# Four convolution layers on 16 images: how the last stage recomputes and loads what it needs

## The chip, the core and the metric

The kernel runs on one core of one Trainium2 chip. Its engines are TensorE (PE, matrix products, with a separate row PEld for its weight loads), VectorE (DVE), ScalarE (ACT), GpSimd (POOL) and SyncE (SP); here POOL and SP mainly issue transfers. The metric is the device time of one execution in microseconds (us). A profile is taken of one execution: its span runs from the first to the last instruction, and the execution's own time is a little longer than its span.

## The reference

The input x has 16 images of 64 channels and 128x128 points, in float32. Four layers follow, each a residual on a group-normalised input:

```python
x = x + L0(gn(x))   # gram matrix of the channels, applied to the image, then a 64x64 mix
x = x + L1(gn(x))   # |Scharr x| + |Scharr y|, per channel
x = x + L2(gn(x))   # temporal shift, 3x3 convolution 64 -> 64, bias
x = x + L3(gn(x))   # 3x3 convolution, 1x1 convolution + b, batch norm, leaky ReLU, clip
```

with, in the last one (called x3 below is its input, y its convolution's output):

```python
y = conv(conv(gn(x3), w_bin), w1x1) + b1x1
mean, var = mean(y, axis=(0, 2, 3)), var(y, axis=(0, 2, 3))     # over all 16 images
y = (y - mean) * rsqrt(var + 1e-5) * gamma + beta
out = x3 + clip(where(y >= 0, y, 0.1 * y), 0, 255)
```

The clip at 0 makes the leaky part a plain ReLU. The mean and the variance need y of every image before the first output can be written; so the kernel has a last stage.

## The kernel before

**The main loop.** Images go through the layers as a pipeline, in chunks of R = 8 rows per half image (a half image has 64 rows; channels of the upper half sit on 64 partitions, of the lower half on the other 64). A step of the loop (`for step in range(FIRST - 2, steps)`) handles a pair of chunks of layer 2 or layer 3 of some image, beside the front layers of a later one. Within a step, `ORDER` is a list, written out by hand, of named pieces of work, and each engine gets its instructions in that order; the wrapper `InOrder` keeps the order of the program (all instructions carry its line, L134, in the profile, so rows are told apart by tile names). `planned` says which step is which; `last_one` is the last step with layer 3 in it.

**What layer 3 leaves behind.** `Layer3.combine` sums y into `bn_sum`, and `Layer3.square` its squares into `bn_sq`. For most images `Layer3.store` writes y to memory (`y_d`), 32 transfers per image from SP. For the images in `AGAIN` y is not stored: the last stage convolves x3 again. x3 is stored for all images (`x3_d`), for those in `AGAIN` as two halves, and their normalising coefficients are kept in `kept`.

**The last stage.** `todo` is a list of 128 pieces. A *loaded* piece is an eighth of an image, whole: y and x3 are read (two transfers of 512 KB), y is scaled, shifted and passed through a ReLU on ScalarE, `min(., 255) + x3` is done on VectorE, and the result is written by POOL. A chunk *again* is one chunk of an image in `AGAIN`: only x3 is read (512 KB), normalised on ScalarE (`again_in`, with the border row above; `again_close`, with the border row below, which comes from the next chunk's x3 or from `xe`, a few rows read ahead), convolved on TensorE (`again_products`), and finished by `again_out`.

`again_products` uses weights that already hold the 1x1 convolution (`w3`, from which `rows_of[ky, h]` are views). The array is used as four quadrants of 64x64: two row halves h times two groups g of four output rows. Nine taps (ky, kx) times four quadrants give 36 products of 4 rows, 512 columns (508 for the outer kx), into the PSUM tile `two_again` (two banks, two buffers). In the profile each product has two records and each record its own weight load. `again_out` then reads the sums on ScalarE (ReLU with scale and shift into z, in three pieces, since the second group's halves lie crossed), adds on VectorE and sends two transfers of 256 KB from POOL.

**Landing places.** Buffers that the main loop no longer needs are collected in `room` (37 places of 512 KB over the run). `fetch` takes the next piece of `todo`, one place or two, and issues its loads from SP. It is called from the last steps of the main loop on, and in the last stage while more than 8 places are free. A load into a place waits for the write out of it.

**Order around the change.** When the main loop is done, `mv`, two small products into `bank` and a chain of small VectorE instructions make the scale `sc` and the shifts `sh` and `shb`. In between stands the first `again_in`. Then the loop over `todo` begins: two chunks with eight loaded pieces, then chunks and loaded pieces mixed, and the last six pieces loaded ones.

Of the kernel before, what the change touches and what calls it, by code (L numbers as in the profile page):

```python
# [80 lines left out]
    ],  # L81
}
FIRST, LAG = 15, 10
AGAIN = (3, 4, 5, 6, 7, 8)
CP = 4
GN_EPS = 1e-5
BN_EPS = 1e-5
# [83 lines left out]
def tile_kernel(ctx: ExitStack, tc: tile.TileContext, x, cw_h, w2_t, b2, wbin_t, w1_t, b1, gamma, beta, consts, out):  # L171
# [58 lines left out]
    def cols(o):  # L230
        return slice(o * C, (o + 1) * C)
# [27 lines left out]
    def chunk_tile(name):  # L259
        return ring.tile([P, (R + 2) * W], F32, tag="v", name=name, bufs=4)  # L260
# [879 lines left out]
    def start_of(b):  # L1140
        return FIRST + LAG + NS * b
# [32 lines left out]
    N = R * W  # L1174
    parts = deque((b, q) for b in range(B) if b not in AGAIN for q in range(C * HW // P // N))
    again = deque((b, i) for b in AGAIN for i in range(NS))
    todo, ahead, behind = [], 8, 6
    share = len(parts) - ahead - behind
    for n in range(NS * len(AGAIN)):
        todo.append(("again",) + again.popleft())  # L1180
        while n > 0 and len(todo) - n - 1 < ahead + (n - 1) * share // (NS * len(AGAIN) - 2):
            todo.append(("loaded",) + parts.popleft())
    todo += [("loaded",) + part for part in parts]
    room, loaded, at_hand = deque(), deque(), deque(maxlen=2)

# [39 lines left out]
    def again_in(b, i, t):  # L1225

        n = AGAIN.index(b)
        v = v_again[0].rearrange("p (j w) -> p j w", w=W)
        v_again.rotate(1)
        r = t.rearrange("p (j w) -> p j w", w=W)  # L1230
        if i == 0:
            act.copy(v[lo, 0, :], w0[lo])
            again_norm(n, v[hi, 0, :], xe[hi, n], hi)
        else:
            again_norm(n, v[:, 0, :], at_hand[-1][1][:, R - 1, :])
        again_norm(n, v[:, 1:R + 1, :], r)
        at_hand.append((v, r, b, i))

    v_again = deque()

    for step in range(FIRST - 2, steps):
        now[0] = step
# [39 lines left out]
        for name in ORDER[kind_of(step)]:  # L1282
            if name in acts:
                if acts[name]:
                    acts[name]()
                continue
            if name == "section":
                if stage:
                    section_of_pair()
                section()  # L1290
                continue
            if name in PARTS:
                for b in fronts:
                    run(Front, b, step - FIRST - NS * b, name)
                continue
            phase[0] = q = int(name)
            for b in range(1, B):
                at, n = pace[b]
                if n == 1:
                    run(Gram, b, step - at, q)  # L1300
                elif 0 <= step - at <= 5:
                    live.setdefault((Gram, b), Gram(b)).half(4 * (step - at) + q)

            first = FIRST
            if step == first and q < 3:
                rows_to_columns(1, NS - 3 + q, rows[NS - 3 + q])
            if q == 1 and first + 2 <= step < first + 5:
                weights_of_layer_3(step - first - 2)
            if q == 1 and step == first + 5:
                other_weights()  # L1310
            tick()

            if step == start_of(B - 1) and q == 0:
                slices(xw.rearrange("p w c t -> p (w c t)"), 8)
                slices(xh.rearrange("p a j w -> p (a j w)"), 3)
                rest(xin, "x", [R, W], 2)
                rest(xin, "xr", [C // 8, W], 3)
# [22 lines left out]
    v_again.extend(chunk_tile(f"v_again_{n}") for n in range(2))  # L1340
    rest(ring, "y", [2, CP, W], 2)
    for t in (dA, dB[0], dB[1]):
        slices(t.rearrange("p n j w -> p (n j w)"), 1)
    rest(ring, "v", [(R + 2) * W], 4, 2)
    while len(room) > 1 and fetched[0] < len(todo):
        fetch()

    mv = cpool.tile([P, 2], F32, name="mv")
    dve.tensor_reduce(mv[:, 0:1], bn_sum, axis=AX.X, op=ALU.add)
# [34 lines left out]

    rows_of = {(kk, i): w3[cols(i), slot, :, cols(o)] for slot, i, o, kk in TO_PAIRS}
    def again_close(r_next):

        v, _, b, i = at_hand[-1]  # L1390
        n = AGAIN.index(b)
        if i + 1 == NS:
            act.copy(v[hi, R + 1, :], w0[hi])
            again_norm(n, v[lo, R + 1, :], xe[lo, n], lo)
        else:
            again_norm(n, v[:, R + 1, :], r_next[:, 0:W])

    def again_products():

        v, r, b, i = at_hand[-1]  # L1400
        two = ps_two.tile([P, 2, CP, W], F32, tag="two", name=f"two_again_{b}_{i}")
        order = [(ky, kx) for kx in (1, 0, 2) for ky in range(3)]
        for n, (ky, kx) in enumerate(order):
            o0, o1 = (0, W) if kx == 1 else (1, W) if kx == 0 else (0, W - 1)
            for g in range(2):
                for h in range(2):
                    j = g * CP + ky
                    pe.matmul(
                        two[cols(h if g == 0 else 1 - h), g, :, o0:o1], rows_of[ky, h][:, kx],
                        v[cols(h), j:j + CP, o0 + kx - 1:o1 + kx - 1], start=n == 0, stop=n + 1 == len(order),  # L1410
                    )
        summed.append((two, r, b, i))

    def again_out():

        two, r, b, i = summed.popleft()
        to = out[b].rearrange("c h w -> (c h w)")
        for g in range(2):
            z = ring.tile([P, CP * W], F32, tag="c", name=f"z_{b}_{i}_{g}", bufs=2)
            for o, at in ((slice(0, P), slice(0, P)),) if g == 0 else ((lo, hi), (hi, lo)):  # L1420
                act.activation(z[o], flat(two[at, g]), AF.Relu, bias=shb[at], scale=sc[at, 1:2])
            to_rows = flat(r[:, g * CP:(g + 1) * CP, :])
            dve.scalar_tensor_tensor(to_rows, z, 255.0, to_rows, op0=ALU.min, op1=ALU.add)
        for h in range(2):
            pool.dma_start(halves(to, h, i * R, R), flat(r)[cols(h)])
        room.append(flat(r))

    rows_of = {(kk, i): w3[cols(i), slot, :, cols(o)] for slot, i, o, kk in TO_PAIRS}
    summed, coming = deque(), deque()
# [23 lines left out]
    while summed:  # L1453
        again_out()


# [36 lines left out]
```

## Time and profile before

| | us |
|---|---|
| median of 3 runs (2513.69 to 2517.16) | 2515.8 |
| the profiled execution's own time | 2513.39 |
| its span | 2511.6 |
| PE busy in the span | 2409.6 (96%) |
| DVE busy | 2078.0 (83%) |
| ACT busy | 2083.6 (83%) |
| POOL busy | 699.5 (28%) |
| last instruction of the main loop's products begins | 2103.6 |
| first product of the last stage begins | 2111.3 |
| end of the span | 2511.6 |

The last stage is thus some 400 of 2511.6 us. Its times below are counted from the span's start. In rows of groups, "x3456 | 375.5, 593" means 3456 instructions, in all 375.5 us during which at least one ran, 593 ns each; what follows is the time that the engine stood idle before them, and who ended that. Matmuls run several at once, so their durations do not add up to time. In rows of a stretch, "20.00 (x108)" is an engine's busy time and count there. "PEclk" or the granted clock is the share of its full clock that TensorE had. A DMA row gives the issuing queue and the time from issue to landing.

### The profile page before, as it was taken

The numbers are of one execution on the slowest core, as the hardware profiler recorded it, in microseconds if no ns is written. First come the engines' busy times: TensorE is split into PE (matmuls) and PEld (weight loads), VectorE is DVE, ScalarE is ACT, GpSimd is POOL, SyncE is SP. The second block draws the span as 40 slices with busy tenths as digits, with TensorE's granted clock in tenths as the row PEclk, the third lists the DMA queues.
The fourth block names the chain that finished last, engine by engine and source line by source line (L and its number), as shares of the span: only waits on it lengthen the run. The fifth ranks groups of instructions, "written<-read, shape, count | busy, mean of one in ns | idle before, by whom it ended". The sixth has DMA issues, their size and how long they took to land.

```text
span 2511.6 us, 52876 instructions
## 1 busy us (share of the span) xinstructions
PE 2409.6 (96%) x19286; PEld 936.2 (37%) x19286; DVE 2078.0 (83%) x2811; ACT 2083.6 (83%) x3509; POOL 699.5 (28%) x1254
## 2 busy tenths in 40 slices
PE   7588999999999999999999999999999999999996
PEld 5333343334334343434343434343333332333332
DVE  4998999999999999999999999999999534444333
ACT  4777999999898898898989899988898656778775
POOL 3251313131423232323323232323232201222222
PEclk8688999999999999999999999999999999999998
DMA  8777888887868686858686978786877798999998
GB/s 229 196 191 205 217 221 224 220 221 197 189 178 199 166 210 163 210 160 207 165 212 183 240 202 233 203 214 160 212 188 174 181 257 277 418 417 418 417 410 338
DMA packets 610579, 585.35 MB, mean 233 GB/s; under 512 B 48480, under 2 KB 521984, under 8 KB 610320
## 3 DMA queue, kind: packets, MB, share of 16 engines
q1 hardware_dynamic: 556752, 425.34, 60.6%
q0 software_dynamic: 53568, 156.63, 20.6%
q8 instruction: 153, 2.51, 0.4%
q14 instruction: 106, 0.87, 0.1%
HBM read 321.46 MB, written 243.28 MB: 225 GB/s over the span
## 4 chain that ended last, share of the span: by engine, by line
PE 77%; DMA 9%; DVE 8%; ACT 2%; issue 2%; POOL 1%; SPq 1%; DVEq 0%; ACTq 0%; POOLq 0%
PE two L134 35%; PE one L134 23%; PE two_again L134 9%; PE bank L134 5%; PE po L134 4%; DVE u L134 3%; DMA end_x<-x_d 3%; DVE e L134 2%; DMA xw<-x_d 1%; DMA v<-x_d 1%; PE pg L134 1%; DMA end_e<-x_d 1%; DMA dA<-x_d 1%; DMA xw<-y_d 1%; DMA xh<-x_d 1%
## 5 line engine op out<-in xcount | busy, mean ns | idle before, releaser
L134 PE MATMUL two<-dA,w 64*64 64x512 f32 (+2 forms) x2304 | 532.8, 595 | 0.0
L134 PE MATMUL two_again<-v_again,w 64*64 64x508 f32 (+1 forms) x3456 | 375.5, 593 | 10.3 <-ACT v_again L134 10.3
L134 PE MATMUL one<-v,w 128*64 128x508 f32 (+2 forms) x1600 | 360.4, 583 | 0.3 <-ACT c L134 0.3
L134 PE MATMUL two<-dB,w 64*64 64x512 f32 (+2 forms) x1536 | 354.6, 594 | 0.0
L134 POOL DMA_DIRECT2D v<-x_d x480 | 238.2, 502 | 399.2 <-PE bank L134 143.7
L134 PE MATMUL one<-v,wi 128*64 128x508 f32 (+3 forms) x1536 | 344.1, 581 | 0.7 <-ACT c L134 0.6
L134 DVE SCALAR_TENSOR_TENSOR e<-e 128x1032 f32<-128x1032 f32 (+1 forms) x256 | 312.8, 1222 | 0.0
L134 ACT ACTIVATE xh<-po,co 128x128 f32<-128x128 f32 (+1 forms) x480 | 274.9, 623 | 25.1 <-PE po L134 24.9
L134 PEld LDWEIGHTS two<-dA,w 64*64 64x64 f32 (+1 forms) x2304 | 150.3, 133 | 287.9 <-issue 283.8
L134 PEld LDWEIGHTS two_again<-v_again,w 64*64 64x64 f32 x3456 | 127.3, 134 | 257.8 <-issue 239.0
L134 ACT ACTIVATE v<-x,co 128x1024 f32<-128x1024 f32 (+3 forms) x256 | 205.3, 847 | 4.0 <-POOL co L134 4.0
L134 PE MATMUL po<-x,abd 64*64 64x512 f32 (+1 forms) x1024 | 179.4, 621 | 21.1 <-ACT xh L134 19.0
L134 PEld LDWEIGHTS one<-v,w 128*64 128x64 f32 x1600 | 109.7, 137 | 211.5 <-issue 187.3
L134 POOL DMA_DIRECT2D q<-dB x128 | 66.6, 522 | 425.4 <-PE one L134 110.9
L134 PEld LDWEIGHTS one<-v,wi 128*64 128x64 f32 x1536 | 103.9, 135 | 215.5 <-issue 171.3
L134 DVE SCALAR_TENSOR_TENSOR y<-two,c 128x1024 f32<-128x1024 f32 x128 | 155.9, 1218 | 32.8 <-PE two L134 23.1
L134 ACT ACTIVATE v<-v,co 128x1154 f32<-128x1154 f32 x128 | 172.0, 1344 | 13.3 <-DMA v<-x_d 11.0
L134 DVE TENSOR_TENSOR dB<-v 128x1024 f32<-128x1024 f32 (+1 forms) x128 | 151.9, 1187 | 36.5 <-ACT v L134 30.9
L134 PE MATMUL two<-q,cross 64*64 64x512 f32 (+1 forms) x768 | 177.2, 570 | 2.2 <-DMA q<-dB 1.5
L134 PE MATMUL two<-dA,wi 128*64 128x508 f32 (+1 forms) x768 | 174.9, 589 | 0.0
L134 DVE TENSOR_TENSOR dA<-v 128x1024 f32<-128x1024 f32 x128 | 156.1, 1219 | 19.3 <-ACT v L134 18.0
L134 DVE SCALAR_TENSOR_TENSOR u<-e,co,u 128x1024 f32<-128x1024 f32 x128 | 164.1, 1282 | 5.3 <-DVE u L134 0.5
(228 smaller groups left out, 4331.4 us busy)
## 6 DMA issues: line engine op xcount, KB each, us to landing
x_d<-u SPq DMA_DIRECT2D x256, 256.0 KB, 3.1
x_d<-x SPq DMA_DIRECT2D x490, 128.0 KB, 4.1
xr<-in_x SPq DMA_DIRECT2D x120, 512.0 KB, 5.8
y_d<-y SPq DMA_DIRECT2D x320, 128.0 KB, 3.9
x<-in_x SPq DMA_DIRECT2D x128, 256.0 KB, 4.9
x<-in_x POOLq DMA_DIRECT2D x128, 256.0 KB, 4.8
end_x<-x_d SPq DMA_DIRECT2D x36, 512.0 KB, 18.1
xw<-x_d SPq DMA_DIRECT2D x33, 512.0 KB, 13.5
```

The source lines that it names most:

```text
L134: return self.tc.keep_in_program_order(call(*args, **kwargs))
```

## The change

Seven images are in `AGAIN` instead of six, so the last stage has 56 chunks and 72 loaded pieces (before 48 and 80), and image 9's y is neither stored nor read.

`again_products` makes two output rows of five products instead of six: with weights w0, w1, w2 of the three rows of taps and input rows v0 to v3, w1(v1 + v2) serves both rows; row 0 adds w0 v0 + (w2 - w1) v2, row 1 adds (w0 - w1) v1 + w2 v3. The row sums v1 + v2 (`s_again`) are made by VectorE in `again_in`, the weight differences (`apart_again`, in `wm`) once by POOL. Each product has 2 rows, 256 columns (254). The shared product goes to banks of its own (`ones`, one in `ps_one`, one in `ps_po`). `again_evict` copies it to SBUF on ScalarE (`c_again`, one buffer in the space of `dA`); `again_sum` adds it on VectorE to the other sums, into z; `again_out` makes the ReLU from z in place.

The order is changed too. The first chunk's `again_in` stands in the step after `last_one`, its products directly behind the two small products of the statistics. `todo` begins with two chunks, then mixes 60 loaded pieces evenly with the chunks, and ends with twelve loaded pieces. At a chunk k the loop does: close and products of k-1, sums of k-2, input of k, copies of k-1, output of k-2; at a loaded piece only that piece's work, except at the end. `dA` is no longer a landing place.

```diff
-AGAIN = (3, 4, 5, 6, 7, 8)
+AGAIN = (3, 4, 5, 6, 7, 8, 9)
...
-    todo, ahead, behind = [], 8, 6
-    share = len(parts) - ahead - behind
+    todo, behind = [], 12
+    share = len(parts) - behind
     for n in range(NS * len(AGAIN)):
+        while len(todo) - n < (n - 1) * share // (NS * len(AGAIN) - 2):
+            todo.append(("loaded",) + parts.popleft())
         todo.append(("again",) + again.popleft())
-        while n > 0 and len(todo) - n - 1 < ahead + (n - 1) * share // (NS * len(AGAIN) - 2):
-            todo.append(("loaded",) + parts.popleft())
...
         again_norm(n, v[:, 1:R + 1, :], r)
         at_hand.append((v, r, b, i))
+        dve.tensor_add(s_again[0], v[:, 1:R + 1:2, :], v[:, 2:R + 2:2, :])
...
             if step == last_one - 3 and q == 0:
+                apart_again = wm.rearrange("p k (n c) -> p n k c", n=2)
+                for h in range(2):
+                    for n, ky in enumerate((2, 0)):
+                        pool.tensor_sub(apart_again[cols(h), n], rows_of[ky, h], rows_of[1, h])
...
+            if step == last_one + 1 and q == 0:
+                v_again.extend(chunk_tile(f"v_again_{n}") for n in range(2))
+                aside = dA.rearrange("p n j w -> p (n j w)")
+                s_again.append(aside[:, 0:CP * W].rearrange("p (j w) -> p j w", w=W))
+                c_again.append(aside[:, CP * W:2 * CP * W])
+                again_in(*todo[0][1:], loaded[0][0])
...
-    for t in (dA, dB[0], dB[1]):
+    for t in dB:
...
     pe.matmul(pm[:, 2:4], k("same"), mv, start=True, stop=True)
+    again_close(loaded[1][0])
+    again_products()
...
-    again_in(*todo[0][1:], loaded[0][0])
...
     def again_products():
...
-        order = [(ky, kx) for kx in (1, 0, 2) for ky in range(3)]
-        for n, (ky, kx) in enumerate(order):
+        s = s_again[0]
+        for part in range(5):
+            for kx in (1, 0, 2):
...
+                        if part == 0:
+                            dst, wt, of = ones[g][to, 0:2], rows_of[1, h], s[cols(h), 2 * g:2 * g + 2, at]
+                        else:
+                            n, far = divmod(part - 1, 2)
+                            dst = two[to, g, n:n + 3:2]
+                            wt = rows_of[2 * n, h] if far else apart_again[cols(h), n]
+                            j += ((2, 0), (1, 3))[n][far]
+                            of = v[cols(h), j:j + 3:2, at]
...
+    def again_evict():
+        while evicted:
+            filled.append(c_again[0])
+            for g, one in enumerate(evicted.popleft()):
+                act.copy(c_again[0][:, 2 * g * W:2 * (g + 1) * W], flat(one[:, 0:2]))
+
+    def again_sum():
+        two, r, b, i = summed.popleft()
+        c = filled.popleft()
...
+                dve.tensor_add(
+                    z[o].rearrange("p (j t w) -> p j t w", t=2, w=W),
+                    two[at, g].rearrange("p (j t) w -> p j t w", t=2),
+                    c[at, 2 * g * W:2 * (g + 1) * W].rearrange("p (j w) -> p j w", w=W).unsqueeze(2)
+                    .to_broadcast([P if g == 0 else C, 2, 2, W]),
+                )
...
     def again_out():
...
-                act.activation(z[o], flat(two[at, g]), AF.Relu, bias=shb[at], scale=sc[at, 1:2])
+            act.activation(z, z, AF.Relu, bias=shb, scale=sc[:, 1:2])
...
         if way == "again":
             (t,) = loaded.popleft()
-            if n > 0:
+            if n > 1:
                 again_close(t)
                 again_products()
-                coming.append((b, q, t))
+            if len(summed) > 1:
+                again_sum()
+            if n > 0:
+                again_in(b, q, t)
+            again_evict()
+            if summed_up:
+                again_out()
         else:
...
-            if len(summed) > 1 or summed and n > len(todo) - behind + 1:
+            if n > last_again and n != last_again + 2 and summed:
+                again_sum()
+            again_evict()
+            if summed_up:
                 again_out()
-            if coming:
-                again_in(*coming.popleft())
-            elif n == len(todo) - behind + 1:
+            if n == last_again + 1:
                 again_close(None)
                 again_products()
```

More of the change, by code (lines that the diff above doesn't have):

```diff
@@ L1237, in again_in @@
         at_hand.append((v, r, b, i))
-    v_again = deque()
+        dve.tensor_add(s_again[0], v[:, 1:R + 1:2, :], v[:, 2:R + 2:2, :])
+    v_again, s_again, c_again = deque(), deque(), deque()
+    rows_of = {(kk, i): w3[cols(i), slot, :, cols(o)] for slot, i, o, kk in TO_PAIRS}
     for step in range(FIRST - 2, steps):
@@ L1339, in tile_kernel @@
         tick()
-    v_again.extend(chunk_tile(f"v_again_{n}") for n in range(2))
     rest(ring, "y", [2, CP, W], 2)
-    for t in (dA, dB[0], dB[1]):
+    for t in dB:
         slices(t.rearrange("p n j w -> p (n j w)"), 1)
@@ L1346, in tile_kernel, with again_close, again_products @@
         fetch()
+    def again_close(r_next):
+        v, _, b, i = at_hand[-1]
+        n = AGAIN.index(b)
+        if i + 1 == NS:
+            act.copy(v[hi, R + 1, :], w0[hi])
+            again_norm(n, v[lo, R + 1, :], xe[lo, n], lo)
+        else:
+            again_norm(n, v[:, R + 1, :], r_next[:, 0:W])
+    def again_products():
+        v, r, b, i = at_hand[-1]
+        two = ps_two.tile([P, 2, CP, W], F32, tag="two", name=f"two_again_{b}_{i}")
+        ones = [
+            pool_of.tile([P, CP, W], F32, tag=tag, name=f"one_again_{b}_{i}_{tag}")
+            for pool_of, tag in ((ps_one, "one"), (ps_po, "po"))
+        ]
+        s = s_again[0]
+        for part in range(5):
+            for kx in (1, 0, 2):
+                o0, o1 = (0, W) if kx == 1 else (1, W) if kx == 0 else (0, W - 1)
+                at = slice(o0 + kx - 1, o1 + kx - 1)
+                for g in range(2):
+                    for h in range(2):
+                        to, j = cols(h if g == 0 else 1 - h), g * CP
+                        if part == 0:
+                            dst, wt, of = ones[g][to, 0:2], rows_of[1, h], s[cols(h), 2 * g:2 * g + 2, at]
+                        else:
+                            n, far = divmod(part - 1, 2)
[3 more added lines that the diff above has]
+                            of = v[cols(h), j:j + 3:2, at]
+                        pe.matmul(
+                            dst[:, :, o0:o1], wt[:, kx], of,
+                            start=part < 2 and kx == 1, stop=part in (0, 4) and kx == 2,
+                        )
+        evicted.append(ones)
+        summed.append((two, r, b, i))
@@ new lines, in again_evict @@
+    def again_evict():
[6 more added lines that the diff above has]
+        c = filled.popleft()
+        zs = []
+        for g in range(2):
+            z = ring.tile([P, CP * W], F32, tag="c", name=f"z_{b}_{i}_{g}", bufs=2)
+            for o, at in ((slice(0, P), slice(0, P)),) if g == 0 else ((lo, hi), (hi, lo)):
+                dve.tensor_add(
[3 more added lines that the diff above has]
+                    .to_broadcast([P if g == 0 else C, 2, 2, W]),
+                )
+            zs.append(z)
+        summed_up.append((zs, r, b, i))
@@ new lines, in again_out @@
+    def again_out():
+        zs, r, b, i = summed_up.popleft()
+        to = out[b].rearrange("c h w -> (c h w)")
+        for g in range(2):
+            z = zs[g]
+            act.activation(z, z, AF.Relu, bias=shb, scale=sc[:, 1:2])
+            to_rows = flat(r[:, g * CP:(g + 1) * CP, :])
+            dve.scalar_tensor_tensor(to_rows, z, 255.0, to_rows, op0=ALU.min, op1=ALU.add)
+        for h in range(2):
+            pool.dma_start(halves(to, h, i * R, R), flat(r)[cols(h)])
+        room.append(flat(r))
@@ L1348, in tile_kernel @@
+    summed, summed_up, evicted, filled = (deque() for _ in range(4))
     mv = cpool.tile([P, 2], F32, name="mv")
@@ L1383, in tile_kernel @@
     dve.scalar_tensor_tensor(shb, sc[:, 1:2], b1_sb, sh[:, 1:2], op0=ALU.mult, op1=ALU.add)
[L1387 to L1401, printed above, removed]
-        order = [(ky, kx) for kx in (1, 0, 2) for ky in range(3)]
-        for n, (ky, kx) in enumerate(order):
[L1404 to L1420, printed above, removed]
-                act.activation(z[o], flat(two[at, g]), AF.Relu, bias=shb[at], scale=sc[at, 1:2])
[L1422 to L1429, printed above, removed]
+    last_again = max(n for n, (way, _, _) in enumerate(todo) if way == "again")
     for n, (way, b, q) in enumerate(todo):
@@ L1452, in tile_kernel @@
             fetch()
-    while summed:
-        again_out()
 def kernel(x, L0_conv_conv_w, L2_conv_W, L2_conv_b, L3_conv_w_bin, L3_conv_w1x1, L3_conv_b1x1, L3_conv_gamma,
```

## The prediction

> **What bounds the kernel now.** I read the page's line of granted clock first, then the end of the run in stretches, then the chain of work that ended last, then single rows for prices.
>
> The stretches (columns: span, length, busy time of each engine with its count, granted clock, DMA share, GB/s):
>
> ```profile
> 2060.00:2080.00 20.00, 20.00 (x108) 6.47 (x106) 9.14 (x12) 8.20 (x13) 0.00 (x0) 1.00 0.88 222
> ...
> 2100.00:2120.00 20.00, 13.94 (x80) 4.87 (x80) 10.09 (x26) 13.79 (x19) 2.23 (x4) 0.74 0.91 283
> ```
> ```profile
> 2120.00:2400.00 280.00, 280.00 (x2628) 94.34 (x2624) 116.51 (x129) 222.08 (x281) 68.78 (x127) 1.00 1.03 417
> 2400.00:2480.00 80.00, 78.30 (x730) 27.87 (x723) 29.77 (x35) 59.80 (x75) 18.99 (x35) 1.00 1.02 409
> 2480.00:2500.00 20.00, 8.48 (x60) 2.28 (x54) 8.71 (x9) 10.82 (x14) 4.85 (x9) 0.82 0.94 359
> ```
>
> From 2112 on, TensorE and the DMA engines are both full: 280.00 of 280 us, and 417 GB/s, which no stretch exceeds. VectorE is 42% busy there, ScalarE 79%. The chain says which of the two full resources ends last (start, length, what):
>
> ```profile
> 2111.26 218.38 PE two_again L134 x2016
> ...
> 2330.87 16.38 DMA end_x<-x_d
> 2347.29 0.03 issue
> 2347.32 18.08 DMA end_x<-x_d
> ...
> 2467.65 16.56 DMA xw<-y_d
> ```
>
> TensorE leads until 2330; afterwards it is a row of loads, up to a loaded piece that arrives at 2484 and lets the last products start. The last combine on VectorE (a loaded piece's) ends at 2503.47, and 8.1 us later the span is over. So before ends by DMA, with TensorE some 10 to 15 us behind it. Before the stage, TensorE is full (20.00 of 20), which hides what the change does there.
>
> **1. Products.** Removed: per chunk 36 products of 512 (508) columns, recorded twice, 72 instructions in 18 rounds of four quadrants. Added: 60 products of 256 (254) columns, 30 rounds. A round now takes 0.427 us (bursts of four weight loads start at 2489.57, 2490.00, 2490.43), a chunk 18 x 0.427 = 7.68. For narrow products the near row is the closing of layer 2, products of 127 and 128 columns, each with its own weight load, two quadrants at a time:
>
> ```profile
> 1927.58 0.82 PE L134 MATMUL two<-v,wi 128*64 128x128 f32 x12
> ...
> 1929.54 2.73 PE L134 MATMUL one<-v,w 128*64 128x512 f32 x12
> ```
>
> 36 of them lie between these starts: 1.96 us, 18 pairs of 0.109. That is 0.85 ns a column against 0.83 in the wide rounds, so 256 columns take about 0.215 and a chunk 30 x 0.215 = 6.45. Sum: 56 x 6.45 = 361.2 against 48 x 7.68 = 368.6.
>
> A rule speaks against this. The Trainium skill, "TensorE: Matmul & The Clock Gate", section on packing small matmuls, says that a weight load overlaps running matmuls only where the row group differs. All four quadrants are streaming when the next four loads run (133 ns each), so by the rule a round would cost its stream plus 0.133: today's chunk 18 x 0.560 = 10.1, the new one 30 x 0.348 = 10.4. The trace has 7.68, so here the loads are covered; I take 6.45. The same page's section on the back-to-back gap gives 81 ns a product at 128 columns in a stream with loads, where the isolated gap would be 56. The closing row has no such surcharge, but it has two loads in flight, not four: upper end 0.25 a round, 7.5 a chunk.
>
> **2. Start.** The first chunk's norms and its row sum move one step ahead of the statistics, ScalarE and VectorE being idle there (6.79 us before the last evictions), and its products follow the two statistics products. These end at 2108.15; the first product starts there rather than at 2111.26. The statistics chain keeps its order. TensorE still idles from 2104.2 to 2107.1, so the halved clock remains (0.74 in the stretch above). In before it cost 218.38 - 28 x 7.68 = 3.3 us; I take 3.0, between 2.8 and 4.5. Last product: 2108.15 + 3.0 + 361.2 = 2472.4, where before had 2494.
>
> **3. ScalarE and VectorE.** Removed per chunk: three ScalarE reads of the product banks (0.79 apart: 2.37 for three). Added: two ScalarE copies 128x256, two Relu 128x512 in place, three VectorE sums (one 128x512, two 64x512 that cross the halves) and one row sum. Prices:
>
> ```profile
> L134 ACT COPY xw<-turned 128x512 f32<-128x512 f32 x8 | 4.7, 588 | 20.0 <-DVE xw L134 20.0
> L134 ACT COPY w<-bank 64x192 f32<-64x192 f32 x6 | 1.9, 316 | 2.6 <-PE bank L134 2.5
> L134 ACT ACTIVATE v<-x,co 128x512 f32<-128x512 f32 x16 | 12.8, 802 | 0.0
> L134 ACT ACTIVATE z<-two_again,shb,sc 64x512 f32<-64x512 f32 x96 | 74.3, 774 | 1.9
> ```
> ```profile
> L134 DVE SCALAR_TENSOR_TENSOR xw<-z,xw 128x512 f32<-128x512 f32 x24 | 16.4, 690 | 14.7 <-ACT z L134 14.6
> L134 DVE TENSOR_TENSOR dB<-v 128x768 f32<-128x768 f32 x16 | 15.3, 956 | 2.6 <-ACT v L134 2.6
> ```
>
> A copy of 256 lies between 316 and 588: 0.37. Successive ScalarE starts are 0.10 closer than a duration (2142.59, 2142.98 for a 0.48), VectorE's 0.08 to 0.09. Where the partition half changes there is no such overlap (the z rows). So: copy 0.27 to the next start, Relu 0.71, a loaded Relu 1.13, norms 0.39 + 1.13 + 0.39; sums 0.70 each, row sum 0.61, combines 0.61 and 1.14. With 60/56 loaded pieces per chunk ScalarE needs 5.1 of 6.45 and VectorE 5.2. By count neither is the bound.
>
> By waits they come close. The copies are queued on ScalarE in front of the Relus and the loaded piece's Relu, and they wait for a buffer that exists once: the second copy of chunk k-1 for the sums of k-2, which stand on VectorE behind the last loaded combine, which waits for the loaded Relu, which stands behind the copies. One turn of this loop: 0.04 + 0.27 + 2 x 0.71 + 1.23 + 0.03 + 1.14 + 2.10 = 6.23. Where two loaded pieces follow each other (6 times in 54) it is 1.14 more, mean 6.36. TensorE wants the copies only some 3.6 us later than they come, so a single long turn is absorbed. TensorE sets the pace, by 0.1.
>
> A chunk's next border row is needed only by the last fifth of its products. At the end the last chunk's border stands behind the Relus of the chunk before, 3.9 us after that one's products, in time for the last fifth at 5.2.
>
> **4. DMA.** Image 9 is no longer read from the stored convolution: 8 pieces of 0.524 MB, at 417 GB/s 10.1 us. One buffer (dA) is no longer a landing place: one piece less in advance, 1.3 us back. Net 8.8. In the main loop 32 stores and their SP issues go, under a full TensorE. Two border loads more on SP (12 took 7.5 us, so 1.3) lie there too, as do four subtractions on POOL: its 64x192 copies took 1235 ns, so 5 to 10 us, while POOL has no instruction in 2060 to 2080. If that cover failed it would cost those few us. The order that spreads loaded pieces evenly fills the eight-place reserve more slowly; during that DMA is not full, but before had the like at its end, so I put the net at nothing (-3 to +4).
>
> **5. Tail.** After the last product: sums to 2.35, the Relu to 3.2, the first of nine loaded Relus to 4.3, then nine combines of 1.14: 14.7, to 2487.1, and 8.1 to the end: 2495. By DMA: 2511.6 - 8.8 = 2502.8. DMA is later and decides. The profiled execution itself took 2513.39 and the median of the runs is 2515.8; so the forecast is 2515.8 - 8.8 = 2507.0.
>
> **The rivals.**
> *ScalarE and VectorE set the pace (slower).* The loop over the one copy buffer. For it: the margin is 0.1 us, and no row shows a copy of 256 or a crossing sum. With copies at 0.41, Relus and sums at 0.79: 0.04 + 0.41 + 1.58 + 1.26 + 0.06 + 1.14 + 2.37 = 6.86, mean 7.0, 56 x 0.54 = 30 us behind TensorE's own time: 2525, median 2529. It decides once the mean turn passes 6.45 + (2511.6 - 2495)/56 = 6.74. Against: each row lies near the lower values.
> *Weight loads show (slower).* At 0.25 a round 56 x 7.5 = 420: 2554, median 2558. It eats the gain from 0.225 a round on. Against: the closing row.
> *Cancelling.* A mean turn of 6.65 to 6.8, or a DMA start that is slower by 5 us or more: 2511 to 2521.
> *TensorE's path alone decides (faster still).* The loads run ahead: 2495, median 2499. Against: 417 GB/s is already full.
>
> **How the numbers follow.** Forecast 0.48, TensorE's path 0.06, cancelling 0.18, the loop 0.20, weight loads 0.08. About 0.2% (5 us) is what a measurement of this kernel tells from no change. Faster 0.54, same 0.18, slower 0.28. The likeliest case alone spans 2502 to 2511 (DMA start, clock). The range gives up most of the loop's upper end and the weight loads: 2500 to 2530.
>
> **What would show it.** Rounds of 0.215 and a chunk pitch of 6.45 with TensorE full; a pitch of 6.7 or more with TensorE waiting for the copy or the row sum means the loop; longer rounds at full clock mean the weights. First product near 2108. DMA near 417 GB/s from about 2140 on. The last combine a loaded piece's, near 2490 to 2495. The prediction is wrong if a copy, Relu or sum costs a tenth more than its row, since 56 turns multiply it.

## The result, and the profile after

| | before | after |
|---|---|---|
| median of 18 runs each, us | 2513.59 (2510.55 to 2519.43) | 2520.23 (2516.33 to 2524.51) |
| ratio after / before, 95% interval | | 1.0025 (1.0018 to 1.0033) |
| the profiled execution's own time, its span | 2513.39, 2511.6 | 2520.33, 2518.5 |
| the two statistics products begin | 2107.1 | 2111.1 |
| from there to the end of the span | 404.5 | 407.4 |
| bytes moved in that time (from the trace) | 162.2 MB | 158.0 MB |

The changed kernel is 6.6 us slower; the forecast was 8.8 us faster. It moves 4.2 MB less in its last stage and still needs 2.9 us more for it.

The page of the changed kernel, head and busy times: TensorE has less to do than before (2409.6 us), VectorE 154 us more, ScalarE 13 us more.

```profile
span 2518.5 us, 59953 instructions
...
PE 2396.1 (95%) x22550; PEld 1066.5 (42%) x22550; DVE 2231.9 (89%) x3043; ACT 2096.2 (83%) x3607; POOL 709.3 (28%) x1267
```

The last stage in stretches (span, length, busy time and count of PE, PEld, DVE, ACT, POOL, then granted clock, DMA share, GB/s):

```profile
2100.00:2120.00 20.00, 17.05 (x178) 8.66 (x180) 7.70 (x23) 9.44 (x17) 0.64 (x1) 0.91 0.97 297
2120.00:2140.00 20.00, 20.00 (x379) 14.23 (x372) 16.70 (x22) 16.50 (x25) 4.70 (x9) 1.00 0.96 319
2140.00:2160.00 20.00, 20.00 (x378) 14.24 (x374) 16.75 (x23) 17.02 (x27) 5.17 (x10) 1.00 1.00 368
2160.00:2180.00 20.00, 20.00 (x380) 14.26 (x376) 16.86 (x23) 17.23 (x27) 5.47 (x10) 1.00 1.03 415
2180.00:2200.00 20.00, 20.00 (x380) 14.26 (x376) 16.86 (x23) 15.72 (x25) 4.93 (x9) 1.00 1.03 415
2200.00:2400.00 200.00, 200.00 (x3732) 142.53 (x3728) 167.95 (x221) 169.51 (x261) 52.54 (x96) 1.00 1.03 411
2400.00:2480.00 80.00, 74.31 (x1387) 52.69 (x1376) 66.51 (x87) 64.79 (x98) 21.35 (x39) 0.98 1.02 408
2480.00:2500.00 20.00, 0.00 (x0) 0.00 (x0) 7.54 (x7) 7.91 (x7) 4.31 (x8) 0.50 0.99 405
```

TensorE is full until 2474, and in the last 44 us it has nothing to do, while the transfers go on at 405 GB/s. So transfers decide the end, as forecast (experiment 4 bears it out). But three things in the last column differ from before, where the stretches from 2120 to 2400 had 417, 417, 417, 418, 417: a slow start (319 and 368), then 411 where 417 stood, and the drain is longer.

The end, on VectorE: each of the last combines (start, length, what; in brackets the idle time before and who ended it) waits for its load.

```profile
2501.71 1.23 DVE L134 SCALAR_TENSOR_TENSOR end_xr<-end_e,end_xr 128x1024 f32<-128x1024 f32 x1 [4.08 <-DMA end_xr<-x_d]
2505.45 1.22 DVE L134 SCALAR_TENSOR_TENSOR end_x<-end_xr,end_x 128x1024 f32<-128x1024 f32 x1 [2.52 <-DMA end_x<-x_d]
2508.46 1.23 DVE L134 SCALAR_TENSOR_TENSOR q<-end_u,q 128x1024 f32<-128x1024 f32 x1 [1.79 <-DMA q<-x_d]
```

### The profile page after: what moved, and what is told of

Its sections match the earlier page's. It is cut to its first block, busy times and chain, and to the rows that moved or that the text cites. A ratio compares the mean times of both kernels' runs of the same rounds, so it can differ in the third digit from the quotient of the medians.

```text
span 2518.5 us, 59953 instructions
## 1 busy us (share of the span) xinstructions
PE 2396.1 (95%) x22550; PEld 1066.5 (42%) x22550; DVE 2231.9 (89%) x3043; ACT 2096.2 (83%) x3607; POOL 709.3 (28%) x1267
## 4 chain that ended last, share of the span: by engine, by line
PE 82%; DVE 8%; DMA 4%; issue 2%; ACT 2%; POOL 1%; SPq 1%; DVEq 0%; POOLq 0%; ACTq 0%
PE two L134 36%; PE one L134 23%; PE two_again L134 11%; PE bank L134 4%; PE po L134 4%; DVE u L134 3%; PE one_again_one L134 3%; DVE e L134 2%; DMA v<-x_d 1%; DMA q<-dB 1%; PE pg L134 1%; DMA y_d<-y 1%; SPq L134 1%; DVE dB L134 1%; DVE dA L134 1%
## 5 line engine op out<-in xcount | busy, mean ns | idle before, releaser
L134 DVE SCALAR_TENSOR_TENSOR u<-xh,co,u 128x1024 f32<-128x1024 f32 x128 | 163.9, 1280 | 4.2 <-ACT u L134 4.1
L134 ACT ACTIVATE junk<-x 128x1024 bf16<-128x1024 f32 x128 | 134.6, 1051 | 38.2 <-DVE x L134 38.1
```

Of the source, the lines that this page charges most:

```text
L134: return self.tc.keep_in_program_order(call(*args, **kwargs))
```

## The experiments

Times are compared with the kernel before as run beside each (2513.4 to 2514.6). Differences below are to that one; a single difference is good to some 2 to 3 us (interval of 0.001 on either side).

**1. The reserve of eight places.** The prediction's words for the slow start were that the even order "fills the eight-place reserve more slowly". If a reserve is what holds loads back, a smaller one frees them.

```diff
-        while len(room) > 8 and fetched[0] < len(todo):
+        while len(room) > 2 and fetched[0] < len(todo):
```

> The changed kernel with one number altered: in the last stage the loads go on while more than 2 landing places are free, not 8. Theory (the transfers decide the end, and filling the reserve of eight places from the evenly mixed order starves them for 30 us after the statistics): the stretches 2120 to 2140 and 2140 to 2160 rise from 319 and 368 GB/s to over 400, and the time falls by 5 to 6 us, to about 2514.5. Rival one (the longer drain of twelve loaded pieces is the loss) and rival two (the transfers run at a lower rate throughout): no gain over 2 us, 2518 to 2521. Rival three (TensorE or the loop over the copy buffer sets the end): no change, 2520.

Measured: 2522.04, +8.4, and 301 GB/s from 2120 to 2140. No gain: the theory of the reserve falls. The reason lies in the code, not in the chip. `len(room)` is counted while the program is written out, not while it runs. In the traces SP and POOL issue the same transfers in the same order with 8 and with 2 (2078 and 934 of them), so the reserve can't withhold anything from SP. This run is in effect a repeat of the changed kernel (both 2520 to 2522).

What SP waits for shows what withholds the loads. Its waits between 2100 and 2170 in the changed kernel (us in total, times, longest):

```profile
SPq L134 <- DMA out<-xw: 27.6, 7, 8.7
SPq L134 <- DMA out<-end_xr: 6.2, 2, 4.0
```

A load needs a place, and a place is free when the write out of it has landed. In the even order, chunks and loaded pieces are finished at TensorE's pace, so that three or so places come free in 6.44 us; and after the loads done in advance there is no stock of free places. This is read from the waits and the code; no run changed the number of places alone. The pace by itself is not too low: 5.3 transfers of 0.524 MB a chunk (3.2 loads, 2.1 writes, by the order of `todo`) in 6.44 us would be 434 GB/s, an estimate. What is missing is loads that are queued while the writes run. Why the rate is back at 415 from 2160 on was not tried.

**2. The order of before, at the start only.** Eight loaded pieces behind the first two chunks, all else as changed.

```diff
-    todo, behind = [], 12
-    share = len(parts) - behind
+    todo, ahead, behind = [], 8, 12
+    share = len(parts) - ahead - behind
     for n in range(NS * len(AGAIN)):
-        while len(todo) - n < (n - 1) * share // (NS * len(AGAIN) - 2):
+        while len(todo) - n < (n > 1) * ahead + (n - 1) * share // (NS * len(AGAIN) - 2):
```

> The changed kernel with the order of the kernel before at the start of the last stage: two chunks, then eight loaded pieces, then the even mixture, twelve loaded pieces last. The reserve of eight is left, so it is filled by the first four loaded pieces. Theory (the fill starves the transfers): over 400 GB/s from about 2130 on, and 4 to 6 us less, 2514 to 2516; TensorE stands still for some 4 us behind its second chunk, which costs nothing since it is done 44 us before the end. Rivals (long drain, lower rate, TensorE's pace): 2519 to 2524, the last with 4 us more for TensorE's pause.

Measured: 2514.79, ratio 1.0009 (1.0000 to 1.0017), +1.15: 5.5 us of the 6.6 are back. The stretches:

```profile
2120.00:2140.00 20.00, 16.80 (x304) 13.17 (x300) 17.55 (x22) 16.63 (x25) 5.97 (x11) 1.00 1.02 406
2140.00:2160.00 20.00, 20.00 (x380) 16.97 (x376) 16.71 (x23) 16.65 (x27) 4.95 (x9) 1.00 1.02 413
...
2200.00:2400.00 200.00, 200.00 (x3735) 169.67 (x3728) 166.02 (x220) 165.92 (x257) 50.92 (x93) 1.00 1.02 411
```

TensorE pauses for 3 us (16.80 of 20), which costs nothing since it is done long before the end, and the rate is 406 and 413 where it was 319 and 368. Eight loaded pieces one after another are finished at ScalarE's pace, not TensorE's, and give sixteen places at once. The queue is longer then. In the DMA view of 2120 to 2140 (issue, count, KB each, median us to landing), the changed kernel has

```profile
out<-xw POOLq DMA_DIRECT2D x6, 256.0 KB, 5.7
out<-xw POOLq DMA_DIRECT2D x1, 512.0 KB, 6.3
```

and this one

```profile
out<-end_xr POOLq DMA_DIRECT2D x2, 512.0 KB, 17.2
out<-xw POOLq DMA_DIRECT2D x4, 256.0 KB, 15.5
```

A short time to landing alone does not show that the transfers starve: in the kernel before, the same writes take 6.8 and 8.0 us from 2240 to 2280, at 417 GB/s. The middle still has 411, not 417: that is another cause.

**3. The even order in the kernel before.** The counterpart: nothing but the start's order is changed there.

```diff
-    todo, ahead, behind = [], 8, 6
+    todo, ahead, behind = [], 1, 6
```

> The kernel before (six images, nine products) with only its order altered: one loaded piece, not eight, behind the first two chunks, then the even mixture, six loaded pieces last. Theory (the order starves the loads at the start: landing places come free only as fast as TensorE finishes chunks, so nothing waits in the queue that could fill the transfer engines): 280 to 370 GB/s between 2120 and 2150 instead of 417, and 4 to 6 us more than before, about 2518.5. Rival (the five products, with more instructions to fetch and copies in the loop, are what slows the transfers): no change, 2513 to 2515.

Measured: 2518.08, ratio 1.0018 (1.0012 to 1.0025), +4.7. With nine products and six images the order alone costs what it gave back in experiment 2.

```profile
2120.00:2140.00 20.00, 20.00 (x192) 6.73 (x188) 6.81 (x8) 13.22 (x17) 3.80 (x7) 1.00 0.98 372
2140.00:2160.00 20.00, 20.00 (x196) 6.67 (x189) 7.71 (x10) 16.38 (x21) 4.87 (x9) 1.00 1.00 383
2160.00:2180.00 20.00, 20.00 (x193) 6.66 (x189) 9.70 (x11) 16.68 (x22) 4.89 (x9) 1.00 1.03 417
```

The rate is below 417 for 40 us and then back at 417, which the changed kernel never reaches.

**4. Six images with the new products and order.**

```diff
-AGAIN = (3, 4, 5, 6, 7, 8, 9)
+AGAIN = (3, 4, 5, 6, 7, 8)
```

> The changed kernel with six images convolved in the last stage, not seven: five products, new order, copies and sums as they are. Theory (transfers decide): eight more pieces of 0.524 MB at 405 to 415 GB/s are 10 us more: about 2530; TensorE's last product is 52 us earlier, near 2423. Rival (TensorE or the loop sets the end): 40 to 50 us less, 2470 to 2480. Rival (convolving image 9 again lengthens the main loop by 4 us): 2526, with the statistics at 2107 after the span's start, not 2111.

Measured: 2525.12 (median of four runs), +11.5; the statistics products begin at 2108.4. TensorE's and the loop's pace are out as the bound (they would have given 2480 at most). The 2530 of the theory is missed: the seventh image is worth only 4.9 us here, not 10. The rival that a seventh image lengthens the main loop comes close (2526); how much of it stays over all profiles is told below.

**5. Seven images with the old products.**

```diff
-AGAIN = (3, 4, 5, 6, 7, 8)
+AGAIN = (3, 4, 5, 6, 7, 8, 9)
```

> The kernel before with seven images in the last stage, nine products as before. Theory: TensorE becomes the bound, 56 chunks of 7.68 us and a half-clocked start of 3.3: the last product near 2545, six loaded pieces behind it, time 2560 to 2565. If the loads still decided it would be some 10 us faster than before, 2504. If image 9's place among the convolved ones lengthens the main loop, the statistics begin near 2111 as in the changed kernel; if not, near 2107 as in the kernel before.

Measured: 2564.28, +50.6, as expected of TensorE as the bound. So the seventh image needs the cheaper products. The statistics products begin at 2111.3.

**6. The five products alone.** Six images, and the order of before at both ends; what remains of the change are the products, their copies and sums, and the earlier first chunk.

```diff
-AGAIN = (3, 4, 5, 6, 7, 8, 9)
+AGAIN = (3, 4, 5, 6, 7, 8)
...
-    todo, behind = [], 12
+    todo, ahead, behind = [], 8, 6
```

> The changed kernel with six images and with the whole order of the kernel before (two chunks, eight loaded pieces, even mixture, six loaded pieces last): against the kernel before only the five products, their copies and sums and the earlier start remain. Theory (order at the start 5 to 6 us, slightly slower transfers in the middle 4 us, longer drain 2 to 3 us): the bytes are those of before and the first and third terms are gone, so 2516 to 2519. Rival (the five products cost nothing in transfers): 2513.5. Rival (the five products are the whole loss): 2524.

Measured: 2521.46, ratio 1.0033 (1.0021 to 1.0046), +8.1. The bytes are those of before, the order is that of before, and yet it is as slow as the whole change. TensorE has time to spare (170 of 200 us in the middle), so its pace is not the reason:

```profile
2200.00:2400.00 200.00, 170.29 (x2903) 133.45 (x2898) 140.75 (x182) 136.38 (x208) 45.42 (x83) 0.97 1.02 412
2400.00:2480.00 80.00, 67.59 (x1163) 52.42 (x1160) 55.51 (x72) 56.23 (x86) 17.90 (x33) 1.00 1.02 404
```

**7. The drain.** As experiment 2, with six loaded pieces last instead of twelve (`ahead, behind = 8, 6`).

> The changed kernel with the order of the kernel before at both ends: eight loaded pieces behind the first two chunks, six loaded pieces last, not twelve. Theory (the longer drain costs 2 to 3 us beside the start's 5): 2511.5 to 2513. Rival (the drain costs nothing, transfers end when they end): 2514 to 2515, as with twelve. Rival (TensorE's last product, now later, leaves the drain no time): 2516 or more.

Measured: 2514.85, +1.45, against 2514.79 with twelve. The drain's length costs nothing: the last loads end when all loads end.

**8. Narrow products in the kernel before.** Each product of 4 rows is cut in two of 2 rows; no new sums, no copies, six images, old order.

```diff
-            for g in range(2):
-                for h in range(2):
-                    j = g * CP + ky
-                    pe.matmul(
-                        two[cols(h if g == 0 else 1 - h), g, :, o0:o1], rows_of[ky, h][:, kx],
-                        v[cols(h), j:j + CP, o0 + kx - 1:o1 + kx - 1], start=n == 0, stop=n + 1 == len(order),
-                    )
+            for half, g, h in [(half, g, h) for half in (0, 2) for g in range(2) for h in range(2)]:
+                j = g * CP + ky + half
+                pe.matmul(
+                    two[cols(h if g == 0 else 1 - h), g, half:half + 2, o0:o1], rows_of[ky, h][:, kx],
+                    v[cols(h), j:j + 2, o0 + kx - 1:o1 + kx - 1],
+                    start=n == 0 and half == 0, stop=n + 1 == len(order) and half == 2,
+                )
```

> The kernel before with each product of 4 rows cut into two of 2 rows (72 products a chunk for 36, 256 columns each): same sums, same order, same images, no copies and no row sums. Theory (the narrow products double TensorE's instructions and weight loads, and what fetches them slows the transfers): between 2180 and 2400 some 406 to 413 GB/s instead of 417, about twice as many bytes on the instruction queue, and 3 to 7 us more than before: 2516.5 to 2520.5. Rival (the copies, the sums and the lost landing place slow the transfers): 2513 to 2515.

Measured: 2521.92, ratio 1.0032 (1.0021 to 1.0044), +7.9: as much as the loss of experiment 6, with the width of the products alone. What else experiment 6 has (copies, sums, the place given up, the order within a chunk) is not in this kernel. The kernel before, and this one:

```profile
2160.00:2280.00 120.00, 120.00 (x1132) 40.44 (x1128) 48.72 (x54) 94.48 (x121) 29.09 (x55) 1.00 1.03 417
2280.00:2400.00 120.00, 120.00 (x1132) 40.45 (x1128) 48.55 (x54) 94.42 (x120) 28.48 (x53) 1.00 1.03 416
```
```profile
2160.00:2280.00 120.00, 120.00 (x2244) 79.90 (x2238) 48.39 (x54) 94.06 (x120) 28.47 (x53) 1.00 1.03 415
2280.00:2400.00 120.00, 118.56 (x2212) 79.41 (x2208) 43.83 (x50) 89.77 (x114) 27.26 (x51) 1.00 1.02 404
2200.00:2400.00 200.00, 198.56 (x3700) 132.71 (x3696) 75.99 (x86) 152.43 (x193) 46.00 (x86) 1.00 1.02 408
2400.00:2480.00 80.00, 74.81 (x1376) 53.51 (x1371) 29.65 (x35) 59.56 (x76) 18.37 (x34) 1.00 1.02 403
```

TensorE issues twice the products (from 2200 to 2400, 3700 records for 1880; each product has two) and twice the weight loads, and the transfers fall to 408 and 403 from 417 and 409. The work on VectorE and ScalarE is that of before. The queue that brings instructions moved 2.95 MB for 2.51: 6912 instructions more are 0.44 MB, in 27 packets of 16 KB.

The loss is not a fixed price per product: with the same number of products the rate is 2 GB/s lower until 2280 and 12 GB/s lower behind it. Experiments 6 and 9 (416, then 410) and the changed kernel (415, then 409) have the same step. What begins there is not known. TensorE's own pace is not it: a chunk takes 7.73 us for 7.68, some 2 us over the whole stage, and TensorE waits for loads from about 2380 on.

**9. Without the copies and sums.** Experiment 6 with the rival taken away: ScalarE reads the banks directly, and the shared products are not added.

```diff
-            for g, one in enumerate(evicted.popleft()):
-                act.copy(c_again[0][:, 2 * g * W:2 * (g + 1) * W], flat(one[:, 0:2]))
+            evicted.popleft()
...
-            z = zs[g]
-            act.activation(z, z, AF.Relu, bias=shb, scale=sc[:, 1:2])
+            z = ring.tile([P, CP * W], F32, tag="c", name=f"z_{b}_{i}_{g}", bufs=2)
+            for o, at in ((slice(0, P), slice(0, P)),) if g == 0 else ((lo, hi), (hi, lo)):
+                act.activation(z[o], flat(zs[at, g]), AF.Relu, bias=shb[at], scale=sc[at, 1:2])
```

> The kernel of six images, five products and the order of before, with the two copies and the three sums a chunk taken away; ScalarE reads the product banks as in the kernel before. The shared product is still computed but not added, so that part is left out of the result of the six images. Theory (TensorE's instruction stream): no change against the same kernel with copies and sums, 2519.5 to 2522. Rival (ScalarE's and VectorE's added work): back to the kernel before, 2513 to 2515.

Measured: 2521.42, +7.4, as with them (+8.1). No cost of ScalarE's and VectorE's added work can be told.

**10. Wide products.** If narrow products are the cost, the five products should be made wide. The even output rows of all four row pairs can share one product, 512 columns into one bank, and the odd rows another; even and odd rows then fill the four quadrants that two groups of rows filled before. Only the shared product stays at 256 columns: 24 + 12 products a chunk, 36 as in the kernel before. Images and order are those of experiment 2.

```diff
-        for part in range(5):
+        for part in range(3):
...
-                            n, far = divmod(part - 1, 2)
-                            dst = two[to, g, n:n + 3:2]
-                            wt = rows_of[2 * n, h] if far else apart_again[cols(h), n]
-                            j += ((2, 0), (1, 3))[n][far]
-                            of = v[cols(h), j:j + 3:2, at]
+                            dst = two[to, g]
+                            wt = rows_of[2 * g, h] if part == 2 else apart_again[cols(h), g]
+                            j = ((2, 0), (1, 3))[g][part - 1]
+                            of = v[cols(h), j:j + R - 1:2, at]
...
-                act.copy(c_again[0][:, 2 * g * W:2 * (g + 1) * W], flat(one[:, 0:2]))
+                for o, at in ((slice(0, P), slice(0, P)),) if g == 0 else ((lo, hi), (hi, lo)):
+                    act.copy(c_again[0][o, 2 * g * W:2 * (g + 1) * W], flat(one[at, 0:2]))
...
-            to_rows = flat(r[:, g * CP:(g + 1) * CP, :])
+            to_rows = r[:, g:R:2, :]
```

> Seven images, eight loaded pieces behind the first two chunks, twelve last, and the five products arranged so that four of them cover all four row pairs at once: the even output rows in one bank and the odd in the other, 24 products of 512 columns and 12 of 256 a chunk instead of 60 of 256. One copy more a chunk (the crossed half in two), otherwise the same work. Theory (TensorE's instruction stream slows the transfers): 36 products as in the kernel before, so the rate of before: 2508 to 2512, under both kernels. Rival: 2514 to 2515.5, as with 60 products. Rival (TensorE's pace): rounds of 0.43 make the chunk 12 x 0.427 / 2 + 3 x 0.215 or twice that, 6.4 as now; if it is 7 or more, over 2520.

Measured: 2551.08, +37. A chunk took 7.2 us: the loop over the one copy buffer is now longer than TensorE's 6.4. Its waits from 2200 to 2400:

```profile
ACT dA L134 <- DVE z L134: 37.9, 28, 1.5
PEld one_again_one L134 <- ACT dA L134: 25.2, 26, 1.0
```

The copy waits for the sums of the chunk before, and TensorE's weight loads wait for the copy. This is the prediction's rival, ScalarE and VectorE setting the pace. The third copy (0.37 us) is only part of it: each sum now reads the whole copy buffer, so the first copy waits for all three sums of the chunk before, where in the changed kernel it waited for the first sum only.

**11. Wide products and two copy buffers.** The second buffer is a landing place given up.

```diff
-                c_again.append(aside[:, CP * W:2 * CP * W])
...
-    for t in dB:
-        slices(t.rearrange("p n j w -> p (n j w)"), 1)
+    slices(dB[1].rearrange("p n j w -> p (n j w)"), 1)
+    copies = dB[0].rearrange("p n j w -> p (n j w)")
+    c_again.extend(copies[:, n * CP * W:(n + 1) * CP * W] for n in range(2))
...
+            c_again.rotate(1)
             filled.append(c_again[0])
```

> The arrangement of 36 products a chunk again, with two copy buffers instead of one (the second in a landing place given up, so 35 places). With one buffer a chunk took 7.2 us: the copies waited 1.5 us for the sums of the chunk before, and the shared products waited 1.0 us for the copies. Theory: without that wait the chunk is 6.4 us again, TensorE is done near 2475, and the transfers, with TensorE's instructions as few as in the kernel before, run at 415 to 417 GB/s: 2508 to 2512. Rival (something else in the copies and sums keeps the pace): 7 us a chunk and 2545 to 2550. Rival (instructions are not what slows the transfers): 2514 to 2516.

Measured: 2509.57 (2506.60 to 2514.00), beside 2514.55 for the kernel before: ratio 0.9983 (0.9975 to 0.9992), 5.0 us faster than before and some 11 us faster than the change.

```profile
2180.00:2200.00 20.00, 20.00 (x237) 15.18 (x233) 16.70 (x23) 17.72 (x29) 5.44 (x10) 1.00 1.03 418
2200.00:2400.00 200.00, 200.00 (x2252) 149.90 (x2248) 164.87 (x218) 178.45 (x289) 50.40 (x93) 1.00 1.03 416
2400.00:2480.00 80.00, 75.12 (x833) 54.61 (x824) 65.10 (x87) 67.90 (x109) 20.26 (x37) 1.00 1.03 412
```

A chunk is 6.41 us, and the transfers run at 416 again with 2252 records of products in 200 us.

**12. Fetching or weight loads?** Cutting the products doubled both. Tiny instructions on other engines add to what is fetched, not to the weight loads.

```diff
             room.extend((yt, rt))
+            for n_tiny in range(24):
+                pool.memset(tiny_p, 0.0)
+                if n_tiny < 14:
+                    dve.tensor_copy(tiny[:, 0:1], tiny[:, 1:2])
```

> The kernel before with 24 tiny writes on GpSimd and 14 tiny copies on VectorE behind each loaded piece, 3040 instructions that do nothing useful; products as before. It parts the two things that the cut products doubled together, instructions to fetch and weight loads. If fetching instructions is what slows the transfers, 3040 instructions are 44% of the 6912 that the cut products added: 44% of 7.9 us, 2516 to 2519. If it is the weight loads or the narrow products themselves: no change, 2512.5 to 2515, as long as GpSimd and VectorE, 25% and 40% busy there, take the tiny work in their idle time.

Measured: 2553.43, +39, which answers nothing: a tiny copy on VectorE took 153 ns, 14 of them 2.6 us a piece, so VectorE became the bound where loaded pieces follow each other. TensorE stood still there for 13 us:

```profile
2140.00:2160.00 20.00, 6.98 (x48) 2.01 (x44) 17.54 (x80) 9.25 (x13) 12.53 (x110) 0.66 0.97 354
2200.00:2400.00 200.00, 200.00 (x1880) 66.98 (x1876) 153.14 (x611) 157.24 (x200) 133.29 (x959) 1.00 1.03 415
```

In the undisturbed middle the rate is 415 with some 1400 tiny instructions in 200 us. By the count (1400 for the cut products' 3640) fetching would take 3.4 of the 9 GB/s that those took; 2 are seen, where TensorE and not the transfers sets the pace. That settles nothing.

## Why the prediction was wrong, point by point

The 6.6 us can be followed along a row of kernels, from before to after, each compared with the kernel before as run beside it. Each step is good to some 3 us, and another row would divide them otherwise:

| step | from to | us |
|---|---|---|
| five narrow products, early first chunk | before, experiment 6 | +8.1 |
| the seventh image | experiment 6, 7 | -6.6 |
| twelve loaded pieces last for six | experiment 7, 2 | -0.3 |
| even order at the start | experiment 2, after | +5.5 |
| sum (6.6 but for rounding) | | +6.7 |

**Step 1, the products on TensorE: right.** Rounds of 0.215 and a chunk of 6.45 were forecast. In the chain of the changed kernel the chunks follow each other by 6.44:

```profile
2121.30 5.15 PE two_again L134 x96
...
2127.75 5.15 PE two_again L134 x96
```

Weight loads do not show on TensorE at that pace. What the step left out is what the narrow products do to someone else.

**Step 2, the start: right in kind.** The first product follows the statistics products at 2111.66, 0.54 us after their start. The halved clock was put at 3.0 us and cost 1.7: the second chunk follows the first by 8.2 us, later ones by 6.44 (granted clock from 2100 to 2120: 0.91, before 0.74). Still all is later than forecast, because the main loop ended 4 us later in this execution; how long it takes scatters (statistics products at 2107.1 to 2111.4 in seven profiles with six images, mean 2108.6, and 2108.4 to 2112.4 in seven with seven, mean 2110.5). The last products end at 2474.3, forecast 2472.4.

**Step 3, the loop over the copy buffer: right that TensorE is not held up, and narrower than it said.** Rows of the last stage after (busy us, mean ns, then idle before):

```profile
L134 ACT ACTIVATE z<-z,shb,sc 128x512 f32<-128x512 f32 x112 | 85.3, 810 | 5.1 <-DVE z L134 5.1
L134 DVE TENSOR_TENSOR z<-two_again,dA 64x512 f32<-64x512 f32 x112 | 77.1, 688 | 2.5
...
L134 ACT COPY dA<-one_again_po 128x256 f32<-128x256 f32 x56 | 20.9, 372 | 42.7 <-DVE z L134 42.7
```

Copies of 372 ns, a Relu of 810, sums of 688: the prices taken were 0.37, 0.80 and 0.69. Where ScalarE catches up, its Relus follow by 6.31 (from 2233.09 to 2258.33 in four turns), the turn that was put at 6.23. One turn in nine, where two loaded pieces follow each other, takes 7.45. The mean is 6.44 where 6.36 was forecast: TensorE's own pace, with nothing in hand. The copies wait 42.7 us for sums and TensorE does not notice. Experiment 10 shows how near the edge this is.

**Step 4, the transfers: here it failed, twice.**

First, "so I put the net at nothing (-3 to +4)" for the start. Its size is +5.5 in the changed kernel and +4.7 alone in the kernel before (experiments 2 and 3), above its upper end, though not clear of it with single differences. That the transfers are not full there was right; "DMA near 417 GB/s from about 2140 on" was not (368 until 2160). The reserve that has to fill is not the cause (experiment 1); the waits of SP speak for places that come free chunk by chunk, with no stock of them. The comparison with the kernel before should have been made at the start, where before had its eight loaded pieces, and not with its end.

Second, the step held 417 GB/s fixed. With products of 256 columns it is 404 to 410 from 2280 to 2400, and no term of the sum had that: +8 us with six images (experiments 6, 8 and 9), 6 us with seven (experiment 11 beside experiment 2). Experiment 11 shows it from the other side: with the same seven images and five products, wide, 416 come back.

The two profiles give much the same sizes. The last stage was forecast 8.8 us shorter and is 2.9 us longer, 11.7 apart. Against 417 GB/s the changed kernel misses (98 + 49) x 20 / 417 = 7.0 us of transfers from 2120 to 2160, and against the rates of before (2 x 120 + 7 x 120 + 1 x 80) / 417 = 2.8 us from 2160 to 2480, both estimates; 2 us stay open. The other 4.0 us between the two spans are the main loop's, which scatters as much.

The image's own term, -10.1 + 1.3, measured -6.6 with the order of before and -4.9 with the even one. Part of the rest lies in the main loop: from the last sums of image 8 to those of image 9 (in the traces) the seven profiles with image 9 convolved have 123.7 to 124.3 us, mean 124.0; the seven with it stored 122.4 to 123.6, mean 122.9. So the main loop, where the step put nothing under a full TensorE, cost 1.0 us. Why the interval grows wasn't tried. The remaining 1 to 2 us are within what single differences can tell.

**Step 5, the tail: right in kind.** Transfers are last; TensorE's products were done 44 us ahead. The last combine is a loaded piece's, as forecast, but at 2508.5 and not near 2490 to 2495, since the loads come later. The longer drain was put at nothing, and is (experiment 7).

**The rivals.** The loop and weight loads on TensorE did not come. "Cancelling" named a start slower by 5 us or more and 2511 to 2521; the time lies there, by luck: only with the second loss added to the first, on top of a smaller saving.

## What to carry to other kernels

Where transfers decide the end, cost an edit by what it does to their rate, also if it stands on another engine: cutting the products left TensorE's own time nearly alone (7.73 us a chunk for 7.68) and took 8 us through the transfers. Look at who frees the buffers and when: work that frees many at once belongs in front, so that loads queue up before the slower mixture begins (5.5 and 4.7 us in two kernels). A buffer that exists once is a loop with a length; write that length beside the pace of the bound before adding even one copy to it.

## What the runs showed of the hardware

**Narrow products slow the transfers.** Twice the products, of 256 columns for 512 (3700 records for 1880 in 200 us), with their weight loads, took the rate from 417 to 408 GB/s, at full clock and with nothing else changed (experiment 8). The Trainium skill, "Runtime: NRT & Kernel Launch", section on instruction fetch, says that each engine's instructions are brought in by transfers, in blocks of 16 KB, and that the cost of it is mostly hidden. The blocks agree (27 more for 6912 instructions). From 2167 to 2347 they took 0.9% of the transfer engines' time in experiment 8, against 0.5% before. That difference is about the 2 GB/s lost until 2280, not the 12 lost behind it; all 27 packets, at about 1 us each on one of 16 engines, are 1.7 us (an estimate) of the 7.9. The 4 KB packets of the loads also became slower, 160 to 165 ns for 159 to 160. Whether the fetching, the weight loads or the products do that is open after experiment 12.

**A full DMA share is not a full rate.** In the changed kernel the share stood at 0.96 with 319 GB/s from 2120 to 2140, and at 1.03 with 415 later. In the trace a 4 KB packet takes 160 ns in the full flow; in the slow start it took some 230 ns with loads alone (272 GB/s), and 272 ns from 16 to 18 us after the statistics products with writes alone (225 GB/s). Read the GB/s against the best stretch of the same kernel before calling the transfers full.

**Small instructions are not free in number.** A VectorE copy of one element a partition took 153 ns, a GpSimd write of the same 99 ns.
